# A row of attention exponentials spread over the partitions by two DMAs through DRAM, in place of TensorE transposes

## Chip, cores, metric

One core of a Trainium2 chip. The metric is the time of one execution on the device in microseconds (us), median of three or four runs (the two probe kernels ran once). Each ratio is between runs of the same chip and the same rounds; the batches ran on different chips, on which the kernel before took 1882.6 to 1884.2 us in the median, so a difference between versions of two batches is good to a us or two.

## The reference

32 graphs of 512 nodes with 128 features go through four residual layers, each behind a layer norm and a ReLU: a graph convolution, a gated graph network of five steps, and two graph attention layers (2 and 3). What the change touches is the attention:

```python
h = x @ W                                  # heads
e_src, e_dst = h @ a_src, h @ a_dst        # one number per node
e = leaky_relu(e_src[:, :, None] + e_dst[:, None, :], 0.2)
e = where(edge, e, -inf);  out = softmax(e, axis=-1) @ h
```

Node i attends to node j. With the exponential taken of each node's numbers first, exp of the leaky ReLU becomes a product of a factor of i, which cancels in the softmax, a factor of j, and a maximum of a number of i and a number of j. So for each graph and layer the kernel needs the number of i for all 512 nodes **as a row, the same on all 128 partitions**; the number of j is one per partition.

## The kernel before

Nodes lie on partitions in C = 4 chunks of 128 (P). Cuts are marked with `# ...`.

```python
def gat_heads(b, l):
    # ... transposes of y, gT copied from PSUM on VectorE (L293)
    for c in range(C):                                          # heads product, L296
        nc.tensor.matmul(q[:, c, :D + 3], gT[:, c * P:(c + 1) * P], w_aug[l], start=True, stop=True)
    # ... arg = the three scores per node times rstd (VectorE)
    h = work.tile([P, C, D + 3], F32, name="h_gat", bufs=3)
    nc.scalar.activation(h[:, :, D:D + 3], arg, AF.Exp)         # L301
    # ... h[:, :, :D] = heads scaled
    kept["h_gat", b] = h

def gat_edges(b, l):
    h = kept["h_gat", b]
    row = side_bank()                                           # PSUM
    for c in range(C):                                          # L311
        nc.tensor.transpose(row[:, c, :], h[:, c, D + 2:D + 3].to_broadcast([P, P]), ident)
    e = work.tile([P, C, N], F32, name="e")
    for j in range(C):                                          # the multiply, L314
        nc.vector.scalar_tensor_tensor(e[:, j, :], flat(row), h[:, j, D + 1:D + 2], maskT[l][:, j, :],
                                       op0=ALU.max, op1=ALU.mult)
    kept["e", b] = e
# gat_out: 16 matmuls with e as weights, divide by the row sum, add to x
```

The stages of several graphs are interleaved: a turn holds one step of the gated network (`ggnn_reset`, `ggnn_prod`, `ggnn_back`, `ggnn_update`) and the side stages of other graphs. Five turns make a round; in each round one graph passes layer 2 and an earlier one layer 3. In one turn of a round, layer 2's heads and layer 3's edges meet. A scheduler sets the order of each engine's instructions at build time; in the traces an instruction that waits holds back those behind it on its engine (VectorE's multiply for 8.59 us, below).

The softmax here doesn't subtract the row's maximum and nothing guards it: scores larger than these inputs give would overflow.

## Time and profile before

| | before |
|---|---|
| time, median of three runs | 1884.26 us (1883.15 to 1886.05) |
| span of the profiled run | 1882.5 us |
| TensorE (PE) busy | 1832.7 us, 97% |
| VectorE (DVE) busy | 1039.3 us, 55% |
| granted TensorE clock, mean | 0.992 |
| a round in the steady part | 56.26 us |

The round is read from the result DMAs, one per graph: the first of the 32 starts at 259.3 us, the 26th at 1665.9, 1406.6 us for 25 rounds. The last six graphs run into the end, where rounds get shorter because work runs out. TensorE is the bound, and in the steady part it never waits; the prediction shows the lines for this.

### The profile page before, as it was taken

How to read it: one execution, taken by the hardware profiler on the slowest of the kernel's cores; microseconds unless marked ns; L12 is line 12 of the kernel's file. 1: busy time of each engine (PE TensorE's matmuls, PEld its weight loads, DVE VectorE, ACT ScalarE, POOL GpSimd, SP SyncE). 2: the span in 40 equal slices, each digit the busy share in tenths (PEclk: the TensorE clock that was granted, in tenths of full speed). 3: DMA queues.
4: the chain of work that ended last, by engine and by line, in shares of the span. 5: the costliest groups of instructions: out<-in, count | busy, mean ns of one | idle time of the engine just before them, and what ended most of it. 6: DMA issues, size and time to landing. Idle time of an engine off the chain costs nothing.

```text
span 1882.5 us, 19768 instructions
## 1 busy us (share of the span) xinstructions
PE 1832.7 (97%) x7264; PEld 1052.9 (56%) x7264; DVE 1039.3 (55%) x2814; ACT 723.8 (38%) x1453; POOL 184.7 (10%) x168
## 2 busy tenths in 40 slices
PE   4999999999999999999999999999999999999995
PEld 2444556555556555556555556555555555555664
DVE  3334565555565555555565556565556565555665
ACT  2444443443343444343444344344344344333321
POOL 1101010110010111011111011111011011000000
PEclk9999999999999999999999999999999999999997
DMA  8000000000000000000000000000000000000000
GB/s 218 1 1 1 0 6 7 6 1 6 6 6 7 6 1 6 6 6 7 6 1 6 6 6 6 6 1 6 7 6 7 6 1 6 6 6 6 6 12 12
DMA packets 37056, 19.88 MB, mean 11 GB/s; under 512 B 2528, under 2 KB 36448, under 8 KB 36960
## 3 DMA queue, kind: packets, MB, share of 16 engines
q1 hardware_dynamic: 34368, 17.83, 3.3%
q8 instruction: 57, 0.93, 0.2%
q10 hardware_dynamic: 2592, 0.79, 0.2%
q14 instruction: 39, 0.32, 0.1%
HBM read 10.23 MB, written 8.39 MB: 10 GB/s over the span
## 4 chain that ended last, share of the span: by engine, by line
PE 96%; DVE 2%; DMA 1%; ACT 1%; issue 0%; POOL 0%; SPq 0%; ACTq 0%; DVEq 0%; POOLq 0%
PE prod L189 29%; PE wide L323 12%; PE gate L247 7%; PE cand L252 7%; PE gate L237 7%; PE cand L251 7%; PE gate L238 7%; PE side L189 6%; PE back L184 4%; PE wide L296 3%; PE side L184 2%; PE side L211 2%; PE side L311 1%; DMA x<-in_x_dram 1%; DMA u<-in_L_gnn_u_w_dram 0%
## 5 line engine op out<-in xcount | busy, mean ns | idle before, releaser
L189 PE MATMUL prod<-adjT,h 128*128 128x512 f32 x1280 | 583.2, 594 | 0.0
L189 PEld LDWEIGHTS prod<-adjT,h 128*128 128x128 f32 x1280 | 240.4, 191 | 285.7 <-issue 285.6
L255 DVE TENSOR_TENSOR hv<-hv,hT 128x512 f32<-128x512 f32 x160 | 111.0, 694 | 481.8 <-ACT hv L254 481.8
L170 POOL TENSOR_TENSOR rstd<-ve,mhalf 128x4 f32<-128x4 f32 x128 | 129.4, 1011 | 1557.4 <-DVE off L282 973.0
L323 PEld LDWEIGHTS wide<-h_gat,e 128*128 128x128 f32 x2048 | 238.3, 193 | 20.5 <-issue 11.6
L323 PE MATMUL wide<-h_gat,e 128*128 128x129 f32 x2048 | 241.8, 276 | 3.5 <-DVE o L338 1.5
L231 ACT COPY m<-prod 128x512 f32<-128x512 f32 x160 | 93.1, 582 | 328.6 <-PE prod L189 328.6
L240 ACT ACTIVATE r<-gate,gate_bw 128x512 f32<-128x512 f32 x160 | 109.9, 687 | 277.4 <-PE gate L238 273.6
L314 DVE SCALAR_TENSOR_TENSOR e<-side,h_gat,maskT 128x512 f32<-128x512 f32 x256 | 183.6, 741 | 4.2 <-PE side L311 4.0
L242 DVE SCALAR_TENSOR_TENSOR rh<-r,hT 128x512 f32<-128x512 f32 x160 | 109.4, 684 | 106.2 <-ACT r L240 106.0
L237 PE MATMUL gate<-m,w4T 128*128 128x512 f32 x320 | 164.2, 595 | 2.0 <-ACT m L231 1.5
L247 PE MATMUL gate<-m,w3T 128*128 128x512 f32 x320 | 164.3, 595 | 0.2 <-ACT r L240 0.2
L252 PE MATMUL cand<-rh,u5T 128*128 128x512 f32 x320 | 163.5, 592 | 0.3 <-DVE rh L242 0.3
L238 PE MATMUL gate<-hT,u3T 128*128 128x512 f32 x320 | 163.4, 592 | 0.0
L251 PE MATMUL cand<-m,w5T 128*128 128x512 f32 x320 | 163.4, 592 | 0.0
L254 ACT ACTIVATE hv<-cand,gate_bw 128x512 f32<-128x512 f32 x160 | 109.1, 682 | 97.2 <-PE cand L252 96.8
L258 DVE SCALAR_TENSOR_TENSOR hT<-hv,hT 128x512 f32<-128x512 f32 x160 | 134.7, 842 | 2.6 <-DVE arg L298 0.2
L184 PEld LDWEIGHTS back<-ident,hT 128*128 128x128 f32 x640 | 79.8, 141 | 84.8 <-issue 81.9
L285 ACT ACTIVATE y<-x,off 128x128 f32<-128x128 f32 x256 | 87.7, 393 | 92.7 <-DVE off L282 92.7
L249 ACT ACTIVATE z<-gate,gate_bw 128x512 f32<-128x512 f32 x160 | 109.5, 684 | 27.9 <-PE gate L247 27.9
L164 DVE BATCH_NORM_STATS2 st<-x 128x6 f32<-128x128 f32 x512 | 119.0, 280 | 1.2
L189 PE MATMUL side<-anT,y 128*128 128x512 f32 x256 | 117.4, 601 | 1.9 <-ACT y L179 1.9
(93 smaller groups left out, 1625.8 us busy)
## 6 DMA issues: line engine op xcount, KB each, us to landing
x<-in_x_dram SPq DMA_DIRECT2D x32, 256.0 KB, 5.4
out_dram<-o SPq DMA_DIRECT2D x32, 256.0 KB, 2.2
adj_sb<-in_adj_dram SPq DMA_DIRECT2D x4, 256.0 KB, 5.3
w<-in_L_gnn_w_w_dram ACTq DMA_DIRECT2D x3, 128.0 KB, 5.6
u<-in_L_gnn_u_w_dram ACTq DMA_DIRECT2D x2, 64.0 KB, 4.5
w<-in_L_gnn_W_dram ACTq DMA_DIRECT2D x1, 64.0 KB, 3.0
b<-in_L_gnn_b_dram ACTq DMA_DIRECT2D x1, 64.0 KB, 5.4
w_aug<-in_L_gnn_W_dram ACTq DMA_DIRECT2D x1, 64.0 KB, 3.7
```

The source lines that it names most:

```text
L164: nc.vector.bn_stats(st[:, c, :], xs[b][:, c, :])
L170: nc.gpsimd.tensor_tensor(rstd, ve, mhalf, ALU.pow)
L184: nc.tensor.transpose(p[:, c, :], y[:, c, :], ident)
L189: nc.tensor.matmul(flat(p), h[:, c, :], mT[:, c, :], start=(c == 0), stop=(c == C - 1))
L237: nc.tensor.matmul(flat(p), wT["w4"], m, start=True, stop=False)
L238: nc.tensor.matmul(flat(p), wT["u3"], hT, start=False, stop=True)
L247: nc.tensor.matmul(flat(p), wT["w3"], m, start=False, stop=True, skip_group_check=True)
L251: nc.tensor.matmul(flat(q), wT["w5"], m, start=True, stop=False)
L252: nc.tensor.matmul(flat(q), wT["u5"], rh, start=False, stop=True)
L258: nc.vector.scalar_tensor_tensor(new, hv, 0.5, hT, op0=ALU.mult, op1=ALU.add)
L314: nc.vector.scalar_tensor_tensor(e[:, j, :], flat(row), h[:, j, D + 1:D + 2], maskT[l][:, j, :], op0=ALU.max, op1=ALU.mult)
L323: nc.tensor.matmul(p[:, c, :D + 1], e[:, j, c * P:(c + 1) * P], h[:, j, :D + 1], start=(j == 0), stop=(j == C - 1))
```

## The change

Its intent is to take 256 transposes off the engine that bounds the kernel and let the DMA engines, which are idle, do the spreading: 512 numbers are written to a 2 KB row in DRAM, and the row is read back by all 128 partitions.

```diff
+    dram = ctx.enter_context(tc.tile_pool(name="dram", bufs=1, space=bass.MemoryType.DRAM))
 # gat_heads
-        kept["h_gat", b] = h
+        d = dram.tile([C, P], F32, name="d_row", bufs=4)
+        nc.sync.dma_start(d.rearrange("c p -> p c"), h[:, :, D + 2])
+        row = work.tile([P, C, P], F32, name="row", bufs=3)
+        nc.sync.dma_start(flat(row), d.rearrange("c p -> (c p)").unsqueeze(0).to_broadcast([P, N]))
+        kept["h_gat", b], kept["row", b] = h, row
 # gat_edges
-        h = kept["h_gat", b]
-        row = side_bank()
-        for c in range(C):
-            nc.tensor.transpose(row[:, c, :], h[:, c, D + 2:D + 3].to_broadcast([P, P]), ident)
+        h, row = kept["h_gat", b], kept.pop(("row", b))
```

I call the first DMA the scatter (512 pieces of four bytes, since neighbours in the row come from different partitions) and the second the broadcast.

## The prediction

> **What bounds the kernel now.** I read the page's busy shares first, then the chain that ended last, then the waits of TensorE, then the groups by shape, and at last the timeline of one round.
>
> ```profile
> span 1882.5 us, 19768 instructions
> PE 1832.7 (97%) x7264; PEld 1052.9 (56%) x7264; DVE 1039.3 (55%) x2814; ACT 723.8 (38%) x1453; POOL 184.7 (10%) x168
> PE 96%; DVE 2%; DMA 1%; ACT 1%; issue 0%; POOL 0%; SPq 0%; ACTq 0%; DVEq 0%; POOLq 0%
> ```
>
> TensorE is busy 97% of the span and makes up 96% of the chain; DVE has almost half its time free. The waits view of TensorE for the stretch from 100 to 1780 us lists nothing, and the stretch table has PE busy 1680.00 of those 1680 us: there the time is the sum of TensorE's own slots. Only the first 100 us and the last 80 have idle time. So a TensorE instruction that goes away in the dense stretch is worth its slot, and a new wait costs only what is longer than the slack in front of it.
>
> The slot is not the duration. The group by shape and a piece of the timeline:
>
> ```profile
> L311 PE MATMUL side<-ident,h_gat 128*128 128x128 f32 x256 | 39.3, 276 | 1.6 <-ACT h_gat L301 1.6
> 1030.72 0.60 PE L311 MATMUL side<-ident,h_gat 128*128 128x128 f32 x4
> 1031.16 1.02 PE L237 MATMUL gate<-m,w4T 128*128 128x512 f32 x2
> 1032.02 1.06 PE L296 MATMUL wide<-w_aug,gT 128*128 128x131 f32 x8
> ```
>
> Each of the 256 transposes is recorded as 276 ns and the group covers 39.3 us, but the four that start at 1030.72 are followed by the next matmul at 1031.16: 0.44 us for four, 0.11 us each. The rest lies under the neighbours. In the same way a 512 wide pass holds TensorE for 0.43 us (two in 0.86 us).
>
> **What the Trainium skill says.**
> - "Perfetto Trace Analysis", Identifying the Most-Contended Engine: matmul busy time misleads because matmuls are pipelined. The trace agrees: 276 ns recorded, 110 ns from start to start. I take 110.
> - "DMA: Bandwidth & Descriptors", Anatomy of one DMA: some 2 us per transfer are fixed, mostly the receipt of the last write (it is told for GpSimd's path). The trace has 2.2 us for each 256 KB result written from SyncE's queue.
> - The same page, Two DMAs through the same engine are not ordered: a reader must wait for the first one's completion semaphore. No run before has such a pair; in the order of the changed program the second DMA does wait for the semaphore of the first, so the two latencies add up.
> - "SBUF — State Buffer", Who interferes with whom: a DVE instruction with two SBUF inputs and a GpSimd one that reads SBUF block each other. The trace agrees: L258 took 1.64 us at 1033.50 beside a 1.75 us GpSimd add (L197), and else 0.69.
>
> **The change part by part.**
>
> *Removed.* 64 calls (32 batches, two layers) of four transposes: 256 x 0.109 us = 27.9 us of TensorE slots. Counted with the small waits behind them, the starts of all 256 give 32.5 us, but the extra belongs to the unfilled end and I count it there. One of two shared PSUM banks is held less; as no wait on it shows, that is worth nothing.
>
> *Added.* 128 DMAs on SyncE's queue, which is otherwise idle after the loads (32 result writes): their issue (0.37 us each) and their bytes cost no engine. What counts is how long the row takes from the end of the Exp (L301) to the first use (the mask multiply, L314 before):
>
> ```profile
> L340 SPq DMA_DIRECT2D out_dram<-o x32: 372/372/387, 259.3 to 1879.4; - x32
> DMA to landing us min/median/max: 2.2/2.2/2.3
> ...
> L51 SPq DMA_DIRECT2D adj_sb<-in_adj_dram x4: 328/403/424, 0.7 to 3.8; - x4
> ...
> DMA to landing us min/median/max: 2.9/5.3/5.8
> ```
>
> First DMA: 512 separate 4-byte elements to DRAM. A result write is 512 pieces of 512 bytes in 2.2 us, of which about 0.9 us is data (packets of 27 ns, 32 per engine). Four-byte packets in this trace take 9 ns, so 1.7 to 2.2 us; I take 1.9. Second DMA: 128 pieces of 2 KB into SBUF, the very shape of an adj_sb load, whose first took 2.9 us beside a weight load; alone I put it at 2.6 (estimate). With handovers of 0.15 us the row comes **4.65 us** after the Exp, an estimate from these. Before, through TensorE, it took about 1.2 us when nothing else was in the way.
>
> *Moved.* The order listing shows that the multiplies do not simply wait a turn longer; the scheduler put them at new places. I walk one round, t = 0 at the start of L237 at 1021.22, TensorE packed with slots of 0.86 us per full matmul, 0.44 per four transposes, 0.89 per heads product (L296).
> - Layer 3's row: heads product ends at t = 3.5, Exp ends at 4.2, row at 4.2 + 4.65 = 8.85. DVE reaches the first two multiplies at 8.7 (after the last offset, L177, as in the trace), and in the new order they stand *ahead of* hv (L255) and the copy gT (L293). TensorE needs gT for the next heads product at t = 12.1, and from the end of gT to that matmul goes 0.4 us. From the row on: two multiplies 1.26, hv 0.6, gT 0.69: gT ends at 11.4 and is needed at 11.7. Slack 0.3 us; the row may take **4.96 us** before TensorE waits, and every further us then costs a us in each of some 31 rounds.
> - Layer 2's row: heads product ends at 13.0, Exp at about 15.8 at the latest, row at 20.4. DVE stands idle before its multiply, but the next thing others need from it, hv, cannot start before 19.5, and the state it leads to is wanted by TensorE at 27.8, some four us after it would be ready. Nothing lost.
> - DVE's multiplies now read both operands from SBUF: about 0.69 us (as L256) where the PSUM form took 0.74. 256 x 0.05 = 13 us of DVE, off the path.
>
> *The end.* With nothing else left, the latency is bare:
>
> ```profile
> 1869.49 0.21 ACT L301 ACTIVATE h_gat<-arg 128x12 f32<-128x12 f32 x1 [3.80 <-DVE arg L298]
> 1869.75 1.11 PE L311 MATMUL side<-ident,h_gat 128*128 128x128 f32 x4 [0.64 <-ACT h_gat L301]
> 1870.91 2.72 DVE L314 SCALAR_TENSOR_TENSOR e<-side,h_gat,maskT 128x512 f32<-128x512 f32 x4 [0.28 <-PE side L311]
> 1871.71 6.28 PE L323 MATMUL wide<-h_gat,e 128*128 128x129 f32 x32 [0.84 <-DVE e L314]
> ```
>
> Here Exp to multiply is 1.2 us; with 4.65 it is 3.4 us more. In the pair of batches at 1845 to 1860 both rows are late; in the new order the reciprocal stands behind both sets of multiplies, some 1.5 us more. The groups at 1787 and 1818 have other work, perhaps 1 us together. Sum: +6 us.
>
> *Sum.* 1884.3 - 27.9 + 6 = 1862 us if the row is always in time. For the chance that it takes longer than 4.96 us I add 4 us (spread of 0.6 us about 4.65 gives an average overrun of 0.13 us, times 31 rounds): **1866 us**.
>
> **The rivals.**
> 1. *The row is late in each round.* DVE runs in order, so a late row holds back gT and TensorE with it. For it: the slack is only 0.3 us by my walk; 4-byte writes to DRAM occur nowhere in the trace, and 128 readers of the same 2 KB hardly do (the broadcast bias b0 took 5.4 us, but in the crowd of the loads). Against it: 4-byte packets are short here. A 5.9 us row would cost 0.95 x 31 = 29 us and eat the whole gain (1891 us); 7.5 us would make it some 2 to 3% slower (about 1940 us).
> 2. *The gain is the full group, 39.3 us.* It would give about 1851 us with the end counted. Against it: the start-to-start distance of 0.11 us.
> 3. *GpSimd and DVE block each other more often*, since 256 multiplies now take two SBUF inputs. For it: the 1.64 us of L258. Against it: GpSimd is busy 10%, and a round has one long add. If L258 slipped by a us more in every round, past its slack of about half a us, 15 us would be lost (1881 us).
> 4. *All hidden, and the end costs little*: 1884 - 32 + 3 = 1855 us.
>
> **Range and chances.** Rival 4 and the small end of my terms set the low side, 1854; rival 1 with a row of up to 5.7 us sets the high side, 1890. To be faster by over 2% it would have to come under 1846.6, more than all the slots that go: 0.02. To be slower by over 2% (over 1922) the row must take about 6.9 us: 0.06. Within 2%: 0.92.
>
> **What would show it.** TensorE busy falls by about 28 us or a bit less, and 256 records of the transposes are gone. The DMA view shows the scatter near 1.9 us and the broadcast near 2.6. If the row is in time, TensorE's waits from 100 to 1780 us stay empty; if it is late, they list the heads product (L297 then) waiting for gT some 30 times, and DVE's waits list the multiply waiting for the row's DMA. DVE will show that wait in each round for layer 2 in any case, at no cost. At the end the last multiply waits some 4.6 us after the Exp. Wrong it would be if a DMA took over 3 us, if TensorE waited in the dense stretch, or if the dense stretch shrank by other than about 0.87 us per round of two calls.

## The result, and the profile after

The changed kernel took **2299.1 us** (2297.69 to 2303.1), the kernel before in the same rounds 1884.17: ratio 1.2204, 95% interval 1.2183 to 1.2225. Ratios here are the mean time of one kernel's fast runs over that of the other's of the same rounds, so not quite the ratio of the medians quoted.

The page of the kernel after: span, busy shares, and the chain that ended last by engine and by line.

```profile
span 2297.0 us, 19547 instructions
PE 1917.7 (83%) x7008; PEld 1079.7 (47%) x7008; DVE 1016.9 (44%) x2814; ACT 724.7 (32%) x1453; POOL 172.6 (8%) x168
...
PE 42%; DMA 36%; DVE 19%; issue 2%; ACT 1%; POOL 0%; ACTq 0%; SPq 0%; DVEq 0%; POOLq 0%
```

The 256 transposes are gone from TensorE's count (7264 to 7008). The chain, 96% TensorE before, now lies 36% on the DMAs. TensorE's busy time *rose* by 85 us although it has less to do; most of that is its clock, as shown below.

The DMA issues (last figure: median us from issue to landing), and the group of the multiply (busy, mean ns of one, idle time before it):

```profile
row<-d_row SPq DMA_DIRECT2D x64, 256.0 KB, 4.7
...
d_row<-h_gat SPq DMA_DIRECT2D x64, 2.0 KB, 8.3
...
L317 DVE SCALAR_TENSOR_TENSOR e<-row,h_gat,maskT 128x512 f32<-128x512 f32 x256 | 186.3, 747 | 647.3 <-DMA row<-d_row 647.3
```

8.3 + 4.7 = 13.0 us, where the prediction has 4.65. TensorE's waits between 100 and 2200 us (us in total, times, longest), where the kernel before has none in its steady part:

```profile
PE wide L297 <- DVE gT L294: 207.0, 27, 8.5
PE back L184 <- DVE hT L259: 52.1, 28, 6.0
```

Some 28 rounds lie in this stretch: 7.4 us a round at the heads product and 1.9 us at the transposes back. One round, from the timeline (start, duration; in brackets the idle time before it and its releaser). Here and in the timelines below, lines of other instructions between those shown are left out:

```profile
1268.69 0.21 ACT L302 ACTIVATE h_gat<-arg 128x12 f32<-128x12 f32 x1 [1.31 <-DVE arg L299]
1268.93 0.36 SPq L308 DMA_DIRECT2D d_row<-h_gat  x1
1276.94 0.33 SPq L310 DMA_DIRECT2D row<-d_row  x1
1282.01 1.42 DVE L317 SCALAR_TENSOR_TENSOR e<-row,h_gat,maskT 128x512 f32<-128x512 f32 x2 [8.59 <-DMA row<-d_row]
1283.94 0.69 DVE L294 COPY gT<-side 128x512 f32<-128x512 f32 x1
1284.68 2.11 PE L297 MATMUL wide<-w_aug,gT 128*128 128x131 f32 x8 [7.74 <-DVE gT L294]
1287.27 0.21 ACT L302 ACTIVATE h_gat<-arg 128x12 f32<-128x12 f32 x1 [10.40 <-DVE arg L299]
1300.54 0.75 DVE L317 SCALAR_TENSOR_TENSOR e<-row,h_gat,maskT 128x512 f32<-128x512 f32 x1 [11.91 <-DMA row<-d_row]
1304.57 0.85 PE L184 MATMUL back<-ident,hT 128*128 128x128 f32 x4 [2.48 <-DVE hT L259]
```

Layer 3's exponential ends at 1268.90, the scatter has landed when the broadcast is issued at 1276.94, and the row is there at 1282. VectorE has stood for 8.59 us before the multiply. The copy gT is queued behind it, and TensorE waits 7.74 us for gT. Only the heads product that follows leads to layer 2's exponential at 1287.27, and then that layer's row takes another 13 us, to 1300.54; an update of hT stands behind it, and TensorE waits 2.48 us more. **The two latencies of a round lie one behind the other.**

The stretch table (busy us of PE, PEld, DVE, ACT, POOL with instruction counts; then granted clock, DMA share, GB/s): first the heads product and the matmuls up to the next transposes back, in the kernel before; then, after, the same work split in two, with the idle stretch in front of it.

```profile
1023.80:1027.27 3.47, 3.47 (x16) 1.98 (x14) 3.00 (x16) 0.30 (x2) 0.71 (x1) 1.00 0.00 0
```

```profile
1276.92:1284.68 7.76, 0.02 (x1) 0.00 (x0) 2.67 (x5) 0.00 (x0) 0.67 (x1) 0.76 0.21 34
1284.68:1286.60 1.92, 1.92 (x9) 1.92 (x10) 1.92 (x4) 0.00 (x0) 0.00 (x0) 0.50 0.00 0
1286.60:1289.90 3.30, 3.30 (x9) 1.52 (x9) 2.00 (x5) 0.21 (x1) 0.00 (x0) 0.82 0.08 1
```

After the idle stretch TensorE has half its clock, and the work that took 3.47 us takes 5.07 (1284.68 to the transposes back at 1289.75): 1.6 us lost. After the second wait of this round, 2.48 us long, another 1.7 us are lost (1304.57 to 1308.44 for work of 2.16 us). Other rounds differ: where the second wait is only about 1 us, hardly any clock is lost after it, but more after the first. So the loss is better read from all 25 steady rounds. The same table for them, first the kernel after, then the run with a row in time described below, which has the same work in the same order:

```profile
284.24:1990.61 1706.37, 1470.66 (x5452) 827.51 (x5450) 778.76 (x2166) 558.97 (x1122) 130.45 (x123) 0.92 0.06 12
```

```profile
259.87:1646.01 1386.14, 1385.85 (x5451) 789.38 (x5451) 801.01 (x2166) 556.33 (x1121) 133.13 (x123) 1.00 0.06 15
```

The same matmuls keep TensorE busy 1470.7 us instead of 1385.9, at a mean clock of 0.92 instead of 1.00: 3.4 us a round. The waits of this stretch are 191.7 us for gT and 42.7 us for hT, 7.7 and 1.7 us a round. The three make 12.8 us, and the rounds differ by 12.8 us (68.26 and 55.45): the loss of a steady round is accounted for.

Of the 414.5 us between the two spans, the result DMAs place 24.9 us before the first result (284.2 against 259.3), 299.8 in the 25 steady rounds (68.26 us each, 12.0 more than before) and 89.8 in the end.

### The profile page after: what moved, and what is told of

It reads as the page before. It is cut to its first block, busy times and chain, and to the rows that moved or that the text cites. A ratio compares the mean times of both kernels' runs of the same rounds, so it can differ in the third digit from the quotient of the medians.

```text
span 2297.0 us, 19547 instructions
## 1 busy us (share of the span) xinstructions
PE 1917.7 (83%) x7008; PEld 1079.7 (47%) x7008; DVE 1016.9 (44%) x2814; ACT 724.7 (32%) x1453; POOL 172.6 (8%) x168
## 4 chain that ended last, share of the span: by engine, by line
PE 42%; DMA 36%; DVE 19%; issue 2%; ACT 1%; POOL 0%; ACTq 0%; SPq 0%; DVEq 0%; POOLq 0%
DMA d_row<-h_gat 24%; DMA row<-d_row 12%; PE prod L189 11%; DVE e L317 6%; PE wide L326 6%; PE side L189 5%; PE cand L253 4%; PE gate L248 3%; PE cand L252 3%; PE gate L238 3%; PE gate L239 3%; DVE hv L257 2%; DVE hT L259 2%; PE back L184 2%; DVE hv L256 2%
## 5 line engine op out<-in xcount | busy, mean ns | idle before, releaser
L189 PE MATMUL prod<-adjT,h 128*128 128x512 f32 x1280 | 626.0, 626 | 0.0
L317 DVE SCALAR_TENSOR_TENSOR e<-row,h_gat,maskT 128x512 f32<-128x512 f32 x256 | 186.3, 747 | 647.3 <-DMA row<-d_row 647.3
L189 PEld LDWEIGHTS prod<-adjT,h 128*128 128x128 f32 x1280 | 255.7, 205 | 294.2 <-issue 294.1
L326 PE MATMUL wide<-h_gat,e 128*128 128x129 f32 x2048 | 256.8, 286 | 60.5 <-DVE e L317 47.6
L326 PEld LDWEIGHTS wide<-h_gat,e 128*128 128x128 f32 x2048 | 252.6, 201 | 84.3 <-issue 79.1
L297 PE MATMUL wide<-w_aug,gT 128*128 128x131 f32 x512 | 99.0, 353 | 209.5 <-DVE gT L294 207.8
L256 DVE TENSOR_TENSOR hv<-hv,hT 128x512 f32<-128x512 f32 x160 | 110.9, 693 | 310.0 <-ACT hv L255 310.0
L297 PEld LDWEIGHTS wide<-w_aug,gT 128*128 128x128 f32 x512 | 88.7, 253 | 249.4 <-DVE gT L294 240.4
L248 PE MATMUL gate<-m,w3T 128*128 128x512 f32 x320 | 173.1, 624 | 0.2 <-ACT r L241 0.2
L184 PE MATMUL back<-ident,hT 128*128 128x128 f32 x640 | 101.4, 283 | 62.0 <-DVE hT L259 52.3
L302 ACT ACTIVATE h_gat<-arg 128x12 f32<-128x12 f32 x64 | 13.7, 214 | 342.6 <-DVE arg L299 335.1
```

The lines of the kernel that those rows point to most:

```text
L184: nc.tensor.transpose(p[:, c, :], y[:, c, :], ident)
L189: nc.tensor.matmul(flat(p), h[:, c, :], mT[:, c, :], start=(c == 0), stop=(c == C - 1))
L248: nc.tensor.matmul(flat(p), wT["w3"], m, start=False, stop=True, skip_group_check=True)
L256: nc.vector.tensor_sub(hv, hv, hT)
L326: nc.tensor.matmul(p[:, c, :D + 1], e[:, j, c * P:(c + 1) * P], h[:, j, :D + 1], start=(j == 0), stop=(j == C - 1))
```

## The experiments

The theory: the row's 13 us are the whole loss, passed on by VectorE's fixed order, and most of the 13 us come from four-byte writes into one small stretch of DRAM. Rivals: the loss comes from the *order* that the change gave VectorE, whatever the row does; the DMAs are slow because of the number of pieces, their source, or the traffic.

A caution for all of them: the comparison with the reference does not test the row, and that a version's row is right rests on its indexing alone.

### What the DMAs cost by themselves

Edit: the kernel before, with unread DMAs after layer 2's exponential, eight kinds in turn.

```diff
+        if l == 2:
+            dma_probe(b, h, rstd)      # b % 8 picks the kind
```

> The kernel before, transposes kept, plus transfers that nothing reads, one kind per batch after layer 2's Exp, 4 of each kind; correct result. What it measures is issue to landing in a stretch where TensorE never stalls. Theory A (each 4-byte write to DRAM costs some 13 ns at the memory, and the receipt of the last comes after all): 512 x 4 B to the packed row lands after 8 us as in the changed kernel, the same with the elements 256 B apart or in partition order, 128 x 4 B after 2.5 to 3.5, 128 x 16 B after 2.5 to 3.5, and 512 x 4 B into SBUF after about 2. Theory B (writes to the same memory line collide): elements 256 B apart land after about 2.2, the other two DRAM forms after 8. Theory C (4-byte pieces as such are slow, at the source or in making descriptors): the SBUF target takes 8 too. For the broadcast: theory D (128 readers of one fresh 2 KB row are slow because the memory is still busy with the writes): the broadcast right after the scatter 4.7, a broadcast of an old DRAM row about 2.6 to 3.2, 128 distinct rows about 2.4. Theory E (one hot row is slow in itself): both broadcasts 4.7, distinct rows 2.4. Contention theory (the transfers themselves slow the engines): the time rises by over 10 us; I expect it within 0.3% of before.

Measured, 1884.27 us, as before. Landing times of the row's scatter as the change has it, and of the same with its pieces 256 bytes apart (min/median/max of four each):

```profile
L200 SPq DMA_DIRECT2D d_row<-h_gat x4: 366/367/367, 192.9 to 1540.0; - x4
...
DMA to landing us min/median/max: 8.8/9.5/11.6
```

```profile
L205 SPq DMA_DIRECT2D d_far<-h_gat x4: 377/377/377, 245.8 to 1596.3; - x4
...
DMA to landing us min/median/max: 1.9/1.9/2.5
```

The same 512 pieces from the same source take 9.5 us packed and 1.9 us far apart, in a kernel where nothing waits for them. So it isn't the count, the source or contention from the changed kernel. The other kinds, medians: broadcast of the fresh row 4.4 us, of an old row 3.3; 128 different rows of 2 KB 2.9; 512 pieces of four bytes into SBUF 2.0. A second probe varied the distance.

> The kernel before, with one unread DMA (two in the last case) per graph after layer 2's exponential, eight cases in turn; only the time from issue to landing is of interest. Theory (small writes that fall into the same stretch of DRAM are served one after another): 512 writes of four bytes took 7 to 11 us packed and 1.9 us when 256 bytes apart, so with 8, 16, 32, 64 and 128 bytes between them the time must fall step by step from about 7 to 1.9 us, and reach 1.9 where each stretch holds one write: with a stretch of 64 bytes, 8 bytes apart 4 to 6 us, 16 apart 3 to 4, 32 apart about 2.3, 64 and 128 apart 1.9. 128 writes of four bytes 64 bytes apart: 1.5 to 1.9 us, against 7 to 8 for the packed ones. 128 writes of eight bytes packed: 3 to 5 us. Rival (the time hangs on the size of a write or on the count of writes alone): all 512-write cases alike whatever the distance. Last case, 128 pieces of 16 bytes into one partition of SBUF and a broadcast from it: about 1.5 and 2.5 to 4 us. The kernel's time: 1884, as the first probe.

Measured (1882.64 us for the kernel), medians of four landings, with the first probe's values:

| writes | distance of their starts | us to landing |
|---|---|---|
| 512 x 4 bytes | 4 bytes (packed), laid out chunk by chunk / partition by partition | 9.5 / 7.1 |
| 512 x 4 bytes | 8 bytes | 4.1 |
| 512 x 4 bytes | 16 bytes | 2.7 |
| 512 x 4 bytes | 32, 64, 128, 256 bytes | 2.0, 1.9, 1.9, 1.9 |
| 128 x 4 bytes | 4 bytes (packed) | 7.9 |
| 128 x 4 bytes | 64 bytes | 1.4 |
| 128 x 8 bytes | 8 bytes (packed) | 3.1 |
| 128 x 16 bytes | 16 bytes (packed) | 1.4 |

128 packed writes take about as long as 512: by these probes, it is how many writes fall into the same few dozen bytes that counts. With each doubling of the distance, more than half of what is above 1.9 us goes away, until one or two writes share a stretch of 64 bytes. The packets themselves are not longer: by the packet records in the packed traces, the 512 of a scatter start within 0.37 us (median) and last about 8 ns each, in the kernel after as in the run below with its writes 256 bytes apart. So the extra time lies between the packets and the landing; what in the memory path makes it so, these runs don't show. The last case missed: a broadcast of 256 KB from one SBUF partition took 11.1 us, so SBUF in this form is no way round.

### The row early, the order kept

Edit (the row is wrong): the scatter goes to places 256 bytes apart, and the broadcast reads the first 2 KB of that area.

```diff
-        nc.sync.dma_start(d.rearrange("c p -> p c"), h[:, :, D + 2])
+        d = far[(2 * b + l - 2) % 4]                   # [C, P, 64] in DRAM, filled once
+        nc.sync.dma_start(d[:, :, 0].rearrange("c p -> p c"), h[:, :, D + 2])
...
-        ... d.rearrange("c p -> (c p)") ...
+        ... d.rearrange("c p k -> (c p k)")[0:N] ...
```

> The kernel after with the 512 four-byte writes placed 256 bytes apart, and the broadcast reading the first 2 KB of that area as it stands (so the row is wrong on purpose); every instruction in the same order on every engine as in the kernel after. Theory (the row's 13.0 us are the loss, and four-byte writes packed together are most of it): scatter 1.9, broadcast 3.3, row 5.2 to 5.3 us after the exponential, against the 4.96 us of slack that I worked out: 0.3 us of wait a round for the heads product, no cold clock, so 1862 to 1880 us. Rival (the order that the change gave VectorE, layer 3's multiplies ahead of the copy of gT, costs by itself whatever the row does): 1890 us or more, with waits of 1 us or more a round at the heads product.

Measured: 1887.73 us (1886.47 to 1888.92), ratio 1.0027. TensorE's waits in the steady part were 1.1 us in all, but the first result left at 273.3 us, 14 us later than before, because ScalarE's first normalized features (y) waited 15.2 us for the fill of the areas, 512 KB that stood in SyncE's queue behind the 32 loads of x (not the data behind the fill, as the next expectation has it). So the run missed its number for a reason of its own, and I repeated it with a small fill (2 KB for each area, from GpSimd's queue):

> As the run with the writes 256 bytes apart (row wrong on purpose), but what fills its DRAM area once before the work is 2 KB for each of four areas instead of 512 KB in all; in that run the first graph's data came 15 us late behind the large fill, and the first output left 14 us later than in the kernel before. Theory (the row's lateness is the whole loss of the steady rounds; with a row of 5 us the change would have brought what I predicted): rounds of 55.5 us, first output at 260 us, some 6 us lost at the end, 1870 to 1878 us. If the 1887.7 us of that run were more than its fill, it stays above 1883.

Measured: **1870.19 us** (1869.89 to 1870.8), ratio 0.9929, 95% interval 0.9914 to 0.9944. One round, and TensorE's waits from 300 to 1650 us:

```profile
1013.85 0.21 ACT L307 ACTIVATE h_gat<-arg 128x12 f32<-128x12 f32 x1 [1.31 <-DVE arg L304]
...
1019.08 1.42 DVE L322 SCALAR_TENSOR_TENSOR e<-row,h_gat,maskT 128x512 f32<-128x512 f32 x2 [0.50 <-DMA row<-d_far]
```

```profile
PE wide L302 <- DVE gT L299: 0.3, 1, 0.3
```

The row comes 5.0 us after the exponential (1014.06 to 1019.08), VectorE's order in a round is that of the kernel after, and TensorE waits once. The rounds are 55.45 us, 0.82 shorter than before (predicted 0.87). So the loss is the row's lateness, and for the steady rounds the rest of the prediction's sum holds.

### The order of before, the row slow

Edit: the kernel after, with layer 3's multiplies tied behind the gT copy of layer 2 in VectorE's queue (an order given to the scheduler, no wait).

```diff
-        nc.vector.tensor_copy(gT, flat(p))
+        kept["gT", l] = nc.vector.tensor_copy(gT, flat(p))
...
+        with tc.issue_after(kept["gT", 2].ins) if l == 3 else nullcontext():
             for j in range(C):   # the multiplies
```

> The kernel after with its slow DMAs, layer 3's multiplies queued behind the copy of gT, so VectorE has nearly the order of the kernel before. If the loss were a matter of order alone, 1860 to 1880 us. If the row's 13 us are the loss whatever the order: the row is then wanted 6.8 us after the exponential, 6.2 us too early; the update of hT behind it has some 3 us of slack, so 3.3 us of wait at the transposes back, 1 to 1.5 us at the next product with rh, and some 1.4 us again for layer 2's row, plus 1 to 2 us of slow clock: rounds of 62 to 65 us and 2050 to 2160 us in all. As the kernel after (2299) if the order makes no difference.

Measured: **2298.77 us**, ratio 1.221, the same as the kernel after. The wait for gT is gone and others have taken its place:

```profile
1006.71 0.75 DVE L318 SCALAR_TENSOR_TENSOR e<-row,h_gat,maskT 128x512 f32<-128x512 f32 x1 [7.27 <-DMA row<-d_row]
1007.98 0.16 DVE L299 TENSOR_TENSOR arg<-wide,rstd 128x12 f32<-128x12 f32 x1
1008.93 1.09 PE L184 MATMUL back<-ident,hT 128*128 128x128 f32 x4 [4.59 <-DVE hT L259]
1022.70 2.08 DVE L318 SCALAR_TENSOR_TENSOR e<-row,h_gat,maskT 128x512 f32<-128x512 f32 x3 [10.65 <-DMA row<-d_row]
1027.52 0.89 PE L184 MATMUL back<-ident,hT 128*128 128x128 f32 x4 [3.67 <-DVE rden L330]
```

gT is no longer behind the late row, but the next step towards layer 2's exponential is: arg (L299) is queued behind the first multiply, at 1007.98. So layer 2's row again starts its 13 to 14 us only when layer 3's has come, and the round is 68.0 us as in the kernel after. My 2050 to 2160 missed because I moved only the first of the two stalls. So going back to about the order of before, with the slow row, wins nothing: the order that the change gave VectorE is not the cause. It does not follow that no order helps with a slow row; two further down are 145 and 211 us faster.

### The broadcast alone

Edit: no scatter; the broadcast reads a fixed row of the adjacency (the row is wrong).

> The changed kernel without the scatter: the broadcast reads a fixed row of DRAM and no longer waits for the Exp, so it is long in SBUF when it is wanted (wrong result on purpose). My theory (all of the loss is the wait for the row; the rest of the change is as I reckoned): 1884 - 28 = 1856 us, the end a little shorter too, 1852 to 1858, and no wait of TensorE in the dense stretch. Rival (multiplies that read both inputs from SBUF, GpSimd contention, or the new order cost of themselves): 1875 us or more.

Measured: 1908.04 us (1906.52 to 1909.27), ratio 1.0128. It missed, and is no clean test: with a broadcast that depends on nothing, the scheduler made another order, in which gT stands behind other work, and TensorE waits 1.6 us a round for it while the rows (3.3 us) are never late. It shows that an order alone can cost 1.6 us a round, a fraction of the 12.8.

### Pieces of 16 bytes

Edit: a partition's four numbers lie together in DRAM, so 128 pieces of 16 bytes; the multiply undoes the order by reading the row with a stride.

```diff
-        d = dram.tile([C, P], F32, name="d_row", bufs=4)
-        nc.sync.dma_start(d.rearrange("c p -> p c"), h[:, :, D + 2])
-        row = work.tile([P, C, P], F32, name="row", bufs=3)
+        g = stat.tile([P, C], F32, name="g")
+        nc.scalar.activation(g, arg[:, :, 2], AF.Exp)
+        d = dram.tile([P, C], F32, name="d_row", bufs=4)
+        nc.sync.dma_start(d, g)
+        row = work.tile([P, P, C], F32, name="row", bufs=3)
```

> The changed kernel with the row written as 128 pieces of 16 bytes (a second small Exp makes a packed tile; the multiplies read the row with a stride of four), correct result, and the same order of DVE and TensorE round the multiplies as in the changed kernel. My theory (the loss is the late row, and the scatter of 4-byte pieces makes it late): scatter 1.4 us, broadcast 3.3, row 4.9 to 5.2 us after the first Exp, at the edge of the slack of 4.96: waits of TensorE for gT 0 to 0.5 us a round, time 1858 to 1880 us. Rival (the readers of a freshly written row wait for the memory whatever the piece): broadcast 4.7, row 6.4 us, waits of 1.4 us a round, 1900 us or more. Rival (the strided reads or the new order cost of themselves): multiplies over 0.8 us.

Measured: 1948.98 us (1946.52 to 1950.22), ratio 1.0343. Scatter 1.4 us, broadcast 4.0; 350 of the 415 us come back by this edit of the scatter. Still TensorE waits for gT:

```profile
PE wide L297 <- DVE gT L294: 53.1, 24, 2.7
...
L319 DVE SCALAR_TENSOR_TENSOR e<-row,h_gat,maskT 128x512 f32<-128x512 f32 x256 | 284.7, 1140 | 151.2 <-DMA row<-d_row 151.1
```

2.2 us a round, about the sum of three parts. The row takes 5.7 us, where the kernel after shows a slack of some 5.4 (4.96 in the prediction; see below): 0.3. Each strided multiply takes 1.14 us instead of 0.75, two of them ahead of gT: 0.8. And the prediction's rival 3 shows in a place where it hurts: between those multiplies and gT, the subtraction hv (L256) took 1.70 us instead of 0.69 in the round looked at (at 1000.28), beside a GpSimd add (L198) of 1.69 us: 1.0. The next run put the multiplies behind gT.

> Correct. Pieces of 16 bytes, multiplies that read the row with a stride (1.14 us instead of 0.74), and layer 3's multiplies queued behind the copy of gT. The row comes 5.7 us after its exponential and is wanted at 6.8, so no row wait; if the 2.2 us a round that the version of 16-byte pieces still waited were for the row's lateness and its two slower multiplies ahead of gT, rounds of 55.5 to 56.5 us and 1868 to 1890 us. If the slower multiplies cost by themselves wherever they stand (3.2 us more a round on VectorE, now in front of rh), rounds of 57 to 58 us and 1905 to 1945 us, waits at the product with rh.

Measured: 1909.65 us (1908.19 to 1910.87), ratio 1.0137; rounds of 56.64 us.

```profile
PE cand L253 <- DVE rh L243: 19.9, 24, 0.8
```

No wait for gT is left, but 0.8 us a round at the product with rh: the rival held, the slower multiplies cost wherever they stand, here ahead of rh. So with pieces of 16 bytes the order decided about 1.4 us a round (58.0 in the run before).

### Multiplies later, with the slow and the fast row

Edits: the multiplies tied behind that turn's update of hT (first run); also one turn later, with a fourth buffer for h (second); and that with pieces of 16 bytes (third).

```diff
-        nc.vector.scalar_tensor_tensor(new, hv, 0.5, hT, op0=ALU.mult, op1=ALU.add)
+        kept["pace"] = nc.vector.scalar_tensor_tensor(new, hv, 0.5, hT, op0=ALU.mult, op1=ALU.add)
...
+        with tc.issue_after(kept["pace"].ins):
             for j in range(C):   # the multiplies
...
-            side.append((span + 3 + 4 * i + k, lambda b, f=f, l=l: f(b, l)))
+            side.append((span + 3 + 5 * i + k + 1 * (k > 1), lambda b, f=f, l=l: f(b, l)))
```

> The changed kernel with its slow DMAs, but the multiplies of a batch are queued on DVE behind the state update (hT) of their turn, so gT and hv no longer stand behind them. Theory (the late row hurts through DVE's fixed order: what stands behind the multiply waits with it): rows as late as before (13 us), no wait of TensorE for gT of 8 us; instead rh stands behind layer 3's multiplies and TensorE waits some 3.5 us a round for it; no or little clock loss, as the idle is shorter: 1960 to 2020 us. Rival (the row's lateness costs its full excess whatever stands behind it): about 2300.

> As x5, and the multiplies and the output product come one turn (about 11.5 us) later, so that some 24 us lie between the Exp and the first multiply; same slow DMAs (8.3 and 4.7 us). Theory: row in time, TensorE dense from 300 to 1650 us, the round of five turns 56.3 - 0.9 = 55.4 us, the end longer by 15 to 30 us because the slow rows are bare there: 1870 to 1890 us. Rival (DMA traffic or SBUF ports slow the engines): a round of over 56.3 us.

> x7 with the 16-byte pieces: round 55.4 us as there, the end shorter, 1858 to 1872 us, about 1% faster than the kernel before.

Measured: 2154.62 (ratio 1.1434), 2087.99 (1.1071) and 2011.6 us (1.0671), all slower than expected. TensorE now waits for rh in each; the first, the second and the third:

```profile
PE cand L253 <- DVE rh L243: 112.2, 22, 10.6
```

```profile
PE cand L253 <- DVE rh L243: 79.9, 22, 4.4
```

```profile
PE cand L253 <- DVE rh L243: 63.2, 22, 2.9
```

In the third the rows are in time (5.9 us, hardly any wait of a multiply), and still it waits 2.9 us a round, because eight strided multiplies stand between the update of hT and rh. So these edits put the waits, or the multiplies, in front of the next thing that TensorE needed.

In the first two, part of the wait has another cause, which the record shows and my expectations missed: both rows go through SyncE's queue. A round of the second:

```profile
1042.15 0.36 SPq L308 DMA_DIRECT2D d_row<-h_gat  x1
1045.80 0.21 ACT L302 ACTIVATE h_gat<-arg 128x12 f32<-128x12 f32 x1 [2.68 <-DVE arg L299]
1051.13 0.33 SPq L310 DMA_DIRECT2D row<-d_row  x1
1051.57 0.38 SPq L308 DMA_DIRECT2D d_row<-h_gat  x1
1063.52 0.33 SPq L310 DMA_DIRECT2D row<-d_row  x1
1068.52 2.74 DVE L318 SCALAR_TENSOR_TENSOR e<-row,h_gat,maskT 128x512 f32<-128x512 f32 x4 [4.08 <-DMA row<-d_row]
1071.91 2.07 PE L253 MATMUL cand<-rh,u5T 128*128 128x512 f32 x2 [4.00 <-DVE rh L243]
```

The second exponential has ended at 1046.01, but its scatter is issued only at 1051.57, right after the first row's broadcast, which stood in the queue until its own scatter had landed. The second row thus comes 22.5 us after its exponential, and the multiply waits 4.08 us for it; issued at once it would have been there some 5.6 us sooner, in time (an estimate from these lines, if it lands as fast beside the first row's transfers). In the first run the queue held the second scatter for 2.6 us (exponential over at 1007.45, issue at 1010.02). No run issued the two rows from different queues.

### Two versions meant to beat both

The first leaves the multiplies contiguous: the mask's columns are permuted once into the order of the 16-byte pieces, and the product reads e with a stride as weights.

```diff
-                nc.tensor.matmul(p[:, c, :D + 1], e[:, j, c * P:(c + 1) * P], h[:, j, :D + 1],
+                nc.tensor.matmul(p[:, c, :D + 1], e[:, j, c::C], h[:, j, :D + 1],
```

> Meant as the best version, correct: the row written in 128 pieces of 16 bytes, the node order of that row taken up by a mask with permuted columns (made once) and by reading e with a stride as TensorE weights, so the multiplies stay contiguous; and layer 3's multiplies queued behind the copy of gT, which gives VectorE the order it has in the kernel before. Theory: scatter 1.4, broadcast 4.1, row 5.7 us after the exponential; in the kernel before's order the first multiply of layer 3 comes some 6.8 us after its exponential and that of layer 2 some 8 us after, so no wait is left and the 27.9 us of transposes come off: 1858 to 1872 us. Rival (reading weights with a stride of 16 bytes slows TensorE's weight loads): out products longer than 3.74 us for 32 passes, and a time above 1885.

Measured: 2115.59 us, ratio 1.1237. No wait of TensorE in the steady part; the rival held. The weight loads, before and then in this run:

```profile
L323 PEld LDWEIGHTS wide<-h_gat,e 128*128 128x128 f32 x2048 | 238.3, 193 | 20.5 <-issue 11.6 <-PE cand L251 6.9 <-DVE e L314 1.7
```

```profile
L333 PEld LDWEIGHTS wide<-h_gat,e 128*128 128x128 f32 x2048 | 486.2, 328 | 30.9 <-issue 15.6 <-PE cand L256 7.2 <-PE gate L243 1.6
```

328 ns instead of 193; their group covers 248 us more, about the 245 us that this version is slower than one with rows in time (2115.6 less 1870.2). The Trainium skill, "SBUF — State Buffer", section "Door 1: The DMA port swizzle", says that SBUF has lines of 16 bytes and that accesses which go to a new line each time pay a penalty. Both strided readers here, four-byte elements 16 bytes apart, agree: 1.7 times as long for the weights, 1.5 for VectorE (1.14 against 0.75 us).

The second version keeps one transpose per row: the 128x4 block becomes 4x128, ScalarE copies it, and it goes to DRAM in four pieces of 512 bytes. Layer 3's multiplies stand behind gT; the last three graphs use the transposes of before.

```diff
-        nc.sync.dma_start(d.rearrange("c p -> p c"), h[:, :, D + 2])
+            t = side_bank()
+            nc.tensor.transpose(t[:C, 0, :], h[:, :, D + 2], ident)
+            s = stat.tile([C, P], F32, name="s_row", bufs=2)
+            nc.scalar.copy(s, t[:C, 0, :])
+            nc.sync.dma_start(d, s)
```

> Meant to beat both kernels, correct: one TensorE transpose of the 128x4 column block instead of four broadcasting ones, a small copy on ScalarE, four pieces of 512 bytes to DRAM and the broadcast back, multiplies contiguous and layer 3's behind the copy of gT; the last three graphs take the transposes of the kernel before, so no row is waited for at the end. Theory: write 1.5 to 2 us and broadcast 4.1 us, with the transpose in TensorE's queue and the copy 1.5 to 3 us before them, row 7 to 9 us after its exponential, up to 2 us later than wanted in layer 3, which the 3 us of slack of hT behind it can take. 6 of 8 transposes a round saved, 0.65 us: rounds of 55.6 us and 1862 to 1874 us. Rival (a row of 8 us is too late in both layers, one behind the other): rounds of 57 to 59 us, 1900 us or more.

Measured: **1874.35 us** (1870.09 to 1874.6), ratio 0.9943, 95% interval 0.9926 to 0.9959. Rounds of 55.81 us, and no wait of TensorE from 300 to 1650 us.

```profile
1026.55 0.20 ACT L302 ACTIVATE h_gat<-arg 128x12 f32<-128x12 f32 x1
...
1029.18 0.32 SPq L316 DMA_DIRECT2D row<-d_row  x1
1032.21 0.75 DVE L328 SCALAR_TENSOR_TENSOR e<-row,h_gat,maskT 128x512 f32<-128x512 f32 x1 [1.62 <-DMA row<-d_row]
```

Row at 5.5 us after the exponential, transpose, copy and write included (they end by 1029.18). It is 0.6% faster than the kernel before, clear of the noise but within the 2% that count as the same; it is the best of the versions whose row is right, and little for the trouble.

## Why the prediction was wrong

- **The failed step is the length of the row**, "I take 1.9" for the first DMA and "2.6 (estimate)" for the second, 4.65 in all. They took 8.3 and 4.7 us, 13.0 in all. For the scatter I counted packet time (9 ns each, 32 to an engine), which the first probe shows to be enough *if the writes lie apart* (1.9 us, just my figure). That packed four-byte writes hold the landing back by some 6 us isn't in packet times (about 8 ns each in the kernel after, too), and the trace of before has no such write to read it from. For the broadcast I took a load of 128 different rows (2.9 us by the probe); 128 readers of one row took 3.3, of a freshly written row 4.4.
- **The path was right.** The prediction said a late row would hold gT and the heads product, beyond 4.96 us, a us for a us. 13.0 - 4.96 = 8.0 us; measured 7.7 a steady round, 7.74 in the round shown. With a row of 5.0 us the wait vanished. The slack was slightly larger than the walk gave: it put 0.4 us between the end of gT and the heads product, which in the trace of before was TensorE still busy with L237; in the round shown it is 0.05 us (1284.63 to 1284.68), so the row could take some 5.4 us.
- **The sum was right for a row in time.** 1862 predicted, 1866 with the allowance for a late row; 1870.2 with a row of 5.0 us. A round gave 0.82 us of the 0.87. The end was mis-sized at +6: from the 26th result on, that run takes 222.0 us against 216.6 before, though its six graphs should have saved 6 x 0.87 = 5.2, so it costs 10.6.
- **Rival 1 is what happened, but was mis-sized too.** My own formula with 13.0 us gives 1862 + 8.04 x 31 = 2111 us. The other 188 us are two terms that I left out. First, layer 2's row, which I wrote off as "Nothing lost": at 13 us, and started only after layer 3's, it costs 1.7 us a round, some 53 us in 31 rounds. Second, the clock: after an idle stretch TensorE runs at about half its rate for a while, 3.4 us a round, some 105 us. The rest, about 30 us (41 with the measured 7.7 us in place of 8.04), lies outside the steady rounds; I have not split it further. The Trainium skill warns of this in "TensorE: Matmul & The Clock Gate", section "Why this matters for your kernels": no idle gaps over about 3 us between bursts of matmuls. The trace agrees, with a clock of 0.50 after 7.7 us idle, but here shorter gaps did it too: 0.50 from 1305.21 on, after 2.48 us idle, while waits of about 1 us in other rounds cost hardly any clock.
- **VectorE's multiplies** were put at 0.69 us from SBUF and took 0.747, as long as from PSUM (0.741); harmless.
- **The chances.** I gave 6% to a row over 6.9 us, on packet times and a load of a different kind. The prediction itself noted that four-byte writes to DRAM occur nowhere in the trace; that was a reason for a wide range, with the 0.3 us of slack in front of it.

What stays open: why packed small writes land late, and whether a 13 us latency could be hidden by another order of the whole round; three attempts at it failed, in two of them the second row also waited behind the first in SyncE's queue.

## What to carry to other kernels

A DMA that writes single elements side by side into DRAM can take several times as long as the same pieces spread apart; lay it out so that pieces are larger (16 bytes did here) or lie some 32 bytes or more apart, and measure it alone in an otherwise unchanged kernel before relying on it. When a latency moves from the bounding engine into an in-order queue, ask for each instruction behind the wait who needs it next, and whether the next latency can begin before the first has ended; if not, they add up. The queue that issues the DMAs is such a queue too: a DMA that waits there for another holds up all that is issued behind it, here by up to 5.6 us in the rounds shown. And TensorE here came back at half its clock after waits of 2.5 and of 7.7 us, so a late wait cost more than its length.

## What the Trainium skill lacked or had wrong

- "DMA: Bandwidth & Descriptors", Specifications and "Why small descriptors are slow (HBM only)": small pieces are told by their size alone. The runs show that their neighbourhood decides too: 512 writes of four bytes land after 7.1 to 9.5 us packed, 4.1 us at 8 bytes, 2.7 at 16 and 1.9 to 2.0 from 32 bytes on; 128 of four bytes 7.9 us packed and 1.4 at 64 bytes.
- The same page: no time for many readers of one DRAM row. 128 reads of one 2 KB row took 3.3 us, of a row just written 3.9 to 5.0 in the median of a run, of 128 different rows 2.9; from one SBUF partition 11.1.
- "SBUF — State Buffer": the penalty for a new 16-byte line per access has no figure there. Four-byte elements 16 bytes apart: weight load 328 ns instead of 193, VectorE's multiply 1.14 us instead of 0.75.
